# A message-passing layer: three chunks for the last 724 nodes, and rows fetched by SyncE in place of 16 gathered tiles

## The chip, the core and the metric

The kernel runs on one core of one Trainium2 chip. A core has five engines with a queue of instructions each: TensorE (PE, matrix products; PEld is its weight load), VectorE (DVE), ScalarE (ACT), GpSimd (POOL) and SyncE (SP), which only issues transfers and loads registers. The engines run at the same time, each in its own program order, and wait for one another by semaphores. The metric is the device time of one execution in microseconds, the median of several.

## The reference

There are 12500 nodes with 64 features and 212500 edges, sorted by destination, with 32 features each. What is computed, cut to its core:

```python
msg_in = concatenate([nodes[row], nodes[col], edge_features], axis=-1)   # 64 + 64 + 32
messages = relu(msg_in @ mW1 + mb1) @ mW2 + mb2
aggregated = segment_sum(messages, col, num_segments=12500)
upd = relu(concatenate([nodes, aggregated], axis=-1) @ uW1 + ub1) @ uW2 + ub2
out = layernorm(x + upd)        # per node, eps 1e-5, no scale or shift
```

## The kernel before, in words

All is float32. The edges are taken in 554 groups of 384 (three tiles of 128). For a group GpSimd gathers the source rows of its edges from HBM, one indirect transfer per tile (`gather`, L193), 16 groups ahead of their use into a ring of 20. Beside the rows VectorE writes a one-hot of each edge's destination within a window of 32 nodes (`onehot`, L430).

One **step** of the main loop (`for k in range(G)`) does three things on TensorE, for three different groups: it transposes the rows and one-hots of group k (`turn`, L456), makes the hidden layer of group k - 3 (`hidden`, L482, with weights that hold the window's node terms) and sums the hidden rows of group k - 6 by destination (`sums`, L514). ScalarE copies the transposed block to SBUF, with the sums of the older group in the same instruction (L469); in the last ten steps the sums are copied by themselves (L524). VectorE applies the relu (L493).

Every eighth group is not gathered at all (`COPIED`): 48 of its columns a step are copied from a transposed node table in SBUF, half by VectorE (L666), half by ScalarE (L668).

SyncE issues, in each step, the load of the window's weights four steps ahead of the loop and so seven ahead of `hidden` (`window`, L420) and the store of a group's window sums, 64 rows of 129 numbers (`store`, L445). Every fourth step it loads eight window addresses into registers (L410) and the edge features of four groups (`inputs`, L381); every eighth step a list of columns (`indexes`, L624). The stores go by turns to two tables in HBM.

Nodes are **updated** in chunks. `plan` lists chunks of 512 nodes, each with the group after which no edge to it is left, and one last chunk of 212. Once the sums are `SETTLED` groups past that, `step_update` runs one link of the chunk's chain per group: fetch its rows of both tables (`found`, L536), an idle link, transpose and add the counts (L546) and copy them (L556), the same for the sums (L546, L566), the inner product (L572 to L574), relu (L579), the outer product with the node itself (L586, L588), mean and variance (L595, L596), root (L602), scale (L607, L610) and the output's transfer (L615). All its products use one PSUM buffer (`ups`, one deep). After the loop the links that are left run one after another; the last chunk has all of its links there. Its 212 nodes are taken as 106 partitions by 2.

A stream of rows is prepared in the code before, and is empty: `STREAMS = ()`, so `BY_ROWS` has no groups and `row_numbers` and `row_fetch` do nothing. A second program for inputs that do not fit the plan is behind a branch and is not run here.

Of the kernel before, what the change touches and what calls it, by code (L numbers as in the profile page):

```python
# [10 lines left out]
F32 = mybir.dt.float32  # L11
# [3 lines left out]
AF = mybir.ActivationFunctionType  # L15
# [5 lines left out]
P = 128  # L21
N = 12500
E = 212500
D = 64
DE = 32
H = 128
# [3 lines left out]
W = 32  # L30
TG = 3
GE = TG * P
G = (E + GE - 1) // GE
# [9 lines left out]
ROW = H + 1  # L43
STORED = 2 * W
NT = (E + P - 1) // P
NP = N + 44
CH = 512
# [15 lines left out]
ROW_LEAD = 3  # L63

# [31 lines left out]
BY_ROWS = []  # L96
for _, rate, _ in STREAMS:
    BY_ROWS.append([])
# [9 lines left out]
class Own:  # L108
# [26 lines left out]
def ordered(ctx: ExitStack, tc: tile.TileContext, a, own, ok):  # L135
# [3 lines left out]
    nc = tc.nc  # L139
    x, out = a["x"], a["out"]  # L140
# [4 lines left out]
    ups = ctx.enter_context(tc.tile_pool(name="upd_ps", bufs=1, space=PSUM))  # L145
# [3 lines left out]
    ident, wm = own.ident, own.wm  # L149
    xc = own.xc  # L150
# [65 lines left out]
    eps = const.tile([P, 1], F32, name="eps")  # L216
# [104 lines left out]
    wc = const.tile([H, H], F32, name="wc")  # L321

    store_at, rows_at, indices, columns_by = {}, {}, {}, {}
    rows_by, row_index = {}, {}
    fetched = [[] for _ in STREAMS]
    issuers = {"SP": (nc.sync, ET.SP), "PE": (nc.tensor, ET.PE)}
    x_bytes = x.bitcast(U8).rearrange("n b -> (n b)")
    by_dst = dram.tile([NP, H], F32, name="by_dst")
    tables = [dram.tile([NP + STORED, ROW], F32, name=f"by_node{i}") for i in range(2)]
# [196 lines left out]

        return did, [*relu_by[g], *copy_by[g], *([emptied] if emptied else [])], moved

    def update(base, p, n):

        rows, q = slice(base, base + p * n), p * n

        def found():
            parts = [found_p.tile([P, 4, ROW], F32, name=f"found{i}") for i in range(2)]
            for t, table in zip(parts, tables):
                nc.sync.dma_start(t[:p, :n], table[rows, :].rearrange("(n p) w -> p n w", p=p))  # L536
            return parts

        def settled(parts):
            return parts  # L540

        def joined(parts, w, rows_out):
            ps = ups.tile([H, CH], F32, name="u_ps")[:rows_out]
            for k in range(n):
                for i, t in enumerate(parts):
                    nc.tensor.matmul(ps[:, k * p : (k + 1) * p], t[:p, k, w], ident[:p, :p],  # L546
                                     start=i == 0, stop=i == 1)
            return ps

        def counts(parts):  # L550
            return parts, joined(parts, slice(H, ROW), 1)

        def count_moved(got):
            parts, ps = got
            count = up.tile([1, CH], F32, name="count")
            nc.scalar.activation(count[:, :q], ps[:, :q], AF.Copy)  # L556
            return parts, count

        def all_sums(got):
            parts, count = got  # L560
            return joined(parts, slice(0, H), H), count

        def moved(got):
            ps, count = got
            agg = up.tile([H, CH], F32, name="agg")
            nc.vector.tensor_copy(agg[:, :q], ps[:, :q])  # L566
            return agg, count

        def inner(moved_to):
            agg, count = moved_to  # L570
            u_ps = ups.tile([H, CH], F32, name="u_ps")
            nc.tensor.matmul(u_ps[:, :q], wc, agg[:, :q], start=True, stop=False)  # L572
            nc.tensor.matmul(u_ps[:, :q], per_edge, count[:, :q], start=False, stop=False)  # L573
            nc.tensor.matmul(u_ps[:, :q], ux, xc[: D + 1, rows], start=False, stop=True)  # L574
            return u_ps

        def relu(u_ps):
            u = up.tile([H, CH], F32, name="u")
            nc.scalar.activation(u[:, :q], u_ps[:, :q], AF.Relu)  # L579
            return u  # L580

        def outer(u):
            y = ups.tile([H, CH], F32, name="u_ps")[:, : 4 * D].rearrange("p (n d) -> p n d", n=4)
            for k in range(n):
                at = k * p
                nc.tensor.matmul(y[:p, k], xc[: D + 1, base + at : base + at + p], same,  # L586
                                 start=True, stop=False)
                nc.tensor.matmul(y[:p, k], u[:, at : at + p], u2, start=False, stop=True)  # L588
            return y

        def stats(y):
            parts = up.tile([P, 4, nc.vector.BN_STATS_DIM], F32, name="stats")
            mv = up.tile([P, 4, nc.vector.BN_AGGR_DIM], F32, name="mv")
            for k in range(n):
                nc.vector.bn_stats(parts[:p, k], y[:p, k])  # L595
                nc.vector.bn_aggr(mv[:p, k], parts[:p, k])  # L596
            return y, mv

        def root(ym):
            y, mv = ym  # L600
            rstd = up.tile([P, 4], F32, name="rstd")
            nc.scalar.activation(rstd[:p, :n], mv[:p, :n, 1], AF.Sqrt, bias=eps[:p])  # L602
            return y, mv, rstd

        def scaled(ymr):
            y, mv, rstd = ymr
            nc.vector.reciprocal(rstd[:p, :n], rstd[:p, :n])  # L607
            o = up.tile([P, 4, D], F32, name="o")
            for k in range(n):
                nc.vector.tensor_scalar(  # L610
                    o[:p, k], y[:p, k], mv[:p, k, 0:1], rstd[:p, k : k + 1],
                    ALU.subtract, ALU.mult,
                )
            queue = nc.scalar if base + q == N else nc.sync
            queue.dma_start(out[rows, :].rearrange("(n p) d -> p n d", p=p), o[:p, :n])  # L615

        return [found, settled, counts, count_moved, all_sums, moved, inner, relu, outer, stats, root, scaled]

    def indexes(i):

# [58 lines left out]
    def row_span(n, i):  # L679

        _, rate, steps = STREAMS[n]
        size = ROW_TURNS * rate * steps
# [16 lines left out]
    def row_numbers(n, k):  # L699

        _, rate, steps = STREAMS[n]
        q, r = divmod(k - BEGIN, steps)
# [16 lines left out]
    def row_fetch(n):  # L719

        for q, at in [fetched[n].pop(0) for _ in fetched[n][: STREAMS[n][1]]]:
# [4 lines left out]
            after(i, *([] if p else sided(g)))  # L726
            rows_by.setdefault(g, []).append(i)

    waiting = [(closes, update(base, p, n)) for base, p, n, closes in PLAN]
# [38 lines left out]
    def stored():  # L768

        while unstored:  # L770
            store(unstored.pop(0))
# [4 lines left out]
    weights(SB)  # L776
    inputs(0)
    zeroed()
    projected(0)
    projected(1)  # L780
# [415 lines left out]
```

## Time and profile before

| | |
|---|---|
| median of 3 runs | 1881.22 us (1880.9 to 1882.45) |
| the profiled execution | 1878.41 us |
| its span, first to last instruction | 1876.7 us |
| busy: TensorE, VectorE, ScalarE, GpSimd | 1495.1, 1362.5, 1619.6, 1385.6 us |
| gathers (L193) | 1466, 945 ns each |
| mean granted clock of TensorE | 0.938 |

Busy shares are means over the run and hide the gaps between two instructions that an engine spends on issuing: GpSimd's 74% is not 26% of waiting. SyncE's issues are not counted as busy at all; they stand in the timeline with the letter q (SPq, ACTq), with start and length, and what ended a wait stands in the view of waits. A row of the windows gives the window, its length, then for the chosen line the busy time and the number of instructions, the granted clock, the share of the DMA engines and GB/s.

### The profile page before, as it was taken

The numbers are of one execution on the slowest core, as the hardware profiler recorded it, in microseconds if no ns is written. First come the engines' busy times: TensorE is split into PE (matmuls) and PEld (weight loads), VectorE is DVE, ScalarE is ACT, GpSimd is POOL, SyncE is SP. The second block draws the span as 40 slices with busy tenths as digits, with TensorE's granted clock in tenths as the row PEclk, the third lists the DMA queues.
The fourth block names the chain that finished last, engine by engine and source line by source line (L and its number), as shares of the span: only waits on it lengthen the run. The fifth ranks groups of instructions, "written<-read, shape, count | busy, mean of one in ns | idle before, by whom it ended". The sixth has DMA issues, their size and how long they took to land. (4 is left out here: it accounts for less than half of the span.)

```text
span 1876.7 us, 66058 instructions
## 1 busy us (share of the span) xinstructions
PE 1495.1 (80%) x13157; PEld 1217.2 (65%) x13157; DVE 1362.5 (73%) x14069; ACT 1619.6 (86%) x13169; POOL 1385.6 (74%) x1473
## 2 busy tenths in 40 slices
PE   4777888888788778787787878878878878788785
PEld 4666666676676666666675666767656756666673
DVE  3346888888888887877777778778777777787731
ACT  3368999999999999999999999989999898999830
POOL 7777777777777777777777777777777777777770
PEclk9888999999999999999999989989989899999897
DMA  5544333333333333333333333333332323333330
GB/s 136 130 109 93 62 74 74 64 75 74 64 72 74 65 74 68 63 71 71 63 68 68 65 71 64 69 71 60 72 73 63 71 60 72 70 63 72 71 70 17
DMA packets 195851, 135.48 MB, mean 72 GB/s; under 512 B 61029, under 2 KB 170650, under 8 KB 195434
## 3 DMA queue, kind: packets, MB, share of 16 engines
q1 hardware_dynamic: 147678, 82.58, 19.0%
q0 software_dynamic: 46912, 48.10, 14.4%
q14 instruction: 307, 2.51, 0.5%
q8 instruction: 110, 1.80, 0.4%
q10 hardware_dynamic: 844, 0.48, 0.1%
HBM read 103.03 MB, written 27.95 MB: 70 GB/s over the span
## 5 line engine op out<-in xcount | busy, mean ns | idle before, releaser
L193 POOL DMA_INDIRECT own_rows<-in_x,src_sb x1466 | 1384.8, 945 | 447.9 <-issue 178.6
L668 ACT ACTIVATE own_operands<-own_xc 64x1 f32 x12480 | 1295.1, 189 | 28.4 <-issue 6.7
L666 DVE COPY own_operands<-own_xc 64x1 f32 x12480 | 893.7, 136 | 283.4 <-issue 177.5
L456 PE MATMUL own_ps<-own_ident,own_rows 128*96 128x128 f32 x1661 | 299.2, 292 | 302.6 <-ACT own_operands L668 109.6
L482 PE MATMUL own_pre<-own_wm,own_operands 128*128 128x128 f32 x3322 | 492.4, 288 | 0.0
L514 PE MATMUL own_ps<-own_h,own_rows 128*32 128x128 f32 x3322 | 482.3, 284 | 0.0
L456 PEld LDWEIGHTS own_ps<-own_ident,own_rows 128*96 128x96 f32 x1661 | 171.2, 132 | 424.7 <-ACT own_operands L668 205.4
L482 PEld LDWEIGHTS own_pre<-own_wm,own_operands 128*128 128x128 f32 x3322 | 444.3, 203 | 2.4 <-issue 1.6
L469 ACT ACTIVATE own_operands<-own_ps 96x513 f32<-96x513 f32 (+2 forms) x554 | 321.8, 581 | 129.5 <-PE own_ps L514 108.0
L493 DVE TENSOR_SCALAR own_h<-own_pre 128x384 f32<-128x384 f32 x553 | 300.1, 543 | 172.4 <-PE own_ps L514 134.7
L514 PEld LDWEIGHTS own_ps<-own_h,own_rows 128*32 128x32 f32 x3322 | 336.6, 116 | 6.0 <-issue 0.2
L514 PE MATMUL own_ps<-own_one,own_rows 128*32 128x1 f32 x3322 | 199.1, 175 | 3.2 <-ACT own_operands L469 1.7
L514 PEld LDWEIGHTS own_ps<-own_one,own_rows 128*32 128x32 f32 x3322 | 152.3, 114 | 75.3 <-issue 11.4
L430 DVE TENSOR_TENSOR own_rows<-iota,dlc 128x96 f32<-128x96 f32 x554 | 132.4, 240 | 0.0
L546 PE MATMUL u_ps<-own_ident,found 128*1 128x128 f32 (+2 forms) x784 | 110.6, 298 | 19.8 <-SPq L1155 11.2
L546 PEld LDWEIGHTS u_ps<-own_ident,found 128*1 128x1 f32 (+2 forms) x784 | 80.8, 144 | 39.4 <-issue 16.7
L397 PE MATMUL u_ps<-w1b,own_xc 65*128 65x128 f32 x196 | 34.8, 332 | 39.8 <-DMA own_xc<-in_xT 15.5
L397 PEld LDWEIGHTS u_ps<-w1b,own_xc 65*128 65x128 f32 x196 | 29.5, 230 | 45.6 <-issue 25.4
L400 ACT ACTIVATE t<-u_ps 128x512 f32<-128x512 f32 (+1 forms) x25 | 14.6, 586 | 41.1 <-DMA by_dst<-t 17.6
L586 PE MATMUL u_ps<-same,own_xc 65*128 65x64 f32 (+1 forms) x196 | 39.5, 283 | 1.1 <-ACT u L579 1.1
L588 PE MATMUL u_ps<-u,u 128*128 128x64 f32 (+1 forms) x196 | 38.3, 277 | 0.0
L586 PEld LDWEIGHTS u_ps<-same,own_xc 65*128 65x128 f32 (+1 forms) x196 | 29.9, 192 | 7.1 <-ACT own_operands L668 3.4
(69 smaller groups left out, 328.6 us busy)
## 6 DMA issues: line engine op xcount, KB each, us to landing
own_operands<-in_efT SPq DMA_DIRECT2D x138, 192.0 KB
own_rows<-in_x,src_sb POOLq DMA_INDIRECT x1466
by_node<-own_operands SPq DMA_DIRECT2D x554, 32.2 KB
found<-by_node SPq DMA_DIRECT2D x48, 258.0 KB
own_wm<-by_dst SPq DMA_DIRECT2D x554, 16.0 KB
by_dst<-t SPq DMA_DIRECT2D x24, 256.0 KB
out<-o SPq DMA_DIRECT2D x24, 128.0 KB
own_xc<-in_xT SPq DMA_DIRECT2D x12, 179.2 KB
```

Of the source, the lines that this page charges most:

```text
L193: nc.gpsimd.indirect_dma_start(out=s[:p, j, :D], out_offset=None, in_=x[:, :], in_offset=bass.IndirectOffsetOnAxis(ap=src_sb[:p, g * TG + ...
L397: nc.tensor.matmul(ps[:, j], xc[: D + 1, base + j * P :][:, :P], w1b, start=True, stop=True)
L430: places_by[g] = nc.vector.tensor_tensor(own.s[g % RING][:, :, D:], iota.unsqueeze(1).to_broadcast([P, TG, W]), dlc[:, g * TG : (g + 1) * ...
L456: nc.tensor.transpose(xt[:, j * P : j * P + p], sides[g] if g in sides and j == TG - 1 else s[:p, j, :], ident[:p, :p])
L469: after(nc.scalar.activation(t[r, c : c + n], ps[r, :n], AF.Copy), step))]
L482: nc.tensor.matmul(pre[:p, j, :], t[:, c + j * P : c + j * P + p], wm[g % NW], start=True, stop=True)
L493: relu_by[g] = [nc.vector.tensor_scalar(h, pre, 0.0, None, ALU.max)]
L514: did.append(nc.tensor.matmul(out_ps, s[:p, j, D:], of(j, p), start=j == 0, stop=j == len(sizes) - 1))
L546: nc.tensor.matmul(ps[:, k * p : (k + 1) * p], t[:p, k, w], ident[:p, :p], start=i == 0, stop=i == 1)
L586: nc.tensor.matmul(y[:p, k], xc[: D + 1, base + at : base + at + p], same, start=True, stop=False)
L666: by[engine] = nc.vector.tensor_copy(o, x_at)
L668: by[engine] = nc.scalar.activation(o, x_at, AF.Copy)
```

## The change

Two things are changed.

First, the end. `plan` now lists 23 chunks of 512, two of 256 and the last of 212, so the last 724 nodes are three chunks. `SETTLED` is 1 and not 2. The last chunk is taken in pieces of 128 and 84 nodes; both tables get zeros in the 44 rows behind the last node, so that its fetch reads 128 partitions by 2. Its fetch is issued right after the loop, ahead of the links that other chunks have left. It has a shorter chain of its own (`both`, `both_moved`): sums and counts in one link, each in a PSUM bank of its own, taken from the buffers of the loop, and the product with the nodes' own features ahead of those with counts and sums. Its output goes out in two transfers, one from ScalarE's queue and one from SyncE's. For the other chunks the order of the inner product's three parts is changed in the same way.

Second, `STREAMS = (("SP", 4, 2),)`. In each step from 18 on SyncE issues four transfers of one node row (256 bytes) from HBM to a side tile, and every second step it loads eight row addresses into registers. 128 rows make a tile: the third tile of groups 52, 84, and so on to 532, 16 in all, comes from the side tile and isn't gathered. There are two side tiles. VectorE writes a one-hot into the side tile, and turns row numbers into addresses.

```diff
-SETTLED = 2
+SETTLED = 1
-STREAMS = ()
+STREAMS = (("SP", 4, 2),)
...
-    for e in [c * CH for c in range(1, N // CH + 1)] + [N]:
-        n = e - b
-        chunks.append((b, *((P, n // P) if n % P == 0 else (n // 2, 2)),
-                       next((g for g in range(G) if least(g) >= e), G)))
+    whole = N // CH * CH
+    for e in [*range(CH, whole, CH), whole - CH // 2, whole, N]:
+        chunks.append((b, e - b, next((g for g in range(G) if least(g) >= e), G)))
...
+        for table in tables:
+            for n in range(N, NP, W):
+                m = min(W, NP - n)
+                nc.sync.dma_start(table[n : n + m, :],
+                                  own.st[0][D + W : D + W + m, GE : GE + ROW])
...
+        def bank(i):
+            if final:
+                return (*own.pre, *own.ps)[i][:, :CH]
+            return ups.tile([H, CH], F32, name="u_ps")
...
+        def own_inner(ps):
+            nc.tensor.matmul(ps[:, :q], ux, xc[: D + 1, base : base + q], start=True, stop=False)
+            return ps
...
+        def both(parts):
+            ps = joined(parts, slice(0, H), 0)
+            count = joined(parts, slice(H, ROW), 1)
+            return parts, ps, count, own_inner(bank(2))
...
+            u_ps = begun[0] if begun else own_inner(bank(2))
             nc.tensor.matmul(u_ps[:, :q], per_edge, count[:, :q], start=False, stop=False)
-            nc.tensor.matmul(u_ps[:, :q], ux, xc[: D + 1, rows], start=False, stop=True)
+            nc.tensor.matmul(u_ps[:, :q], wc, agg[:, :q], start=False, stop=True)
...
-            queue = nc.scalar if base + q == N else nc.sync
-            queue.dma_start(out[rows, :].rearrange("(n p) d -> p n d", p=p), o[:p, :n])
+            if final:
+                for k, (p, queue) in enumerate(zip(sizes, (nc.scalar, nc.sync))):
+                    queue.dma_start(out[nodes[k], :], o[:p, k])
...
+    _, (find, *others) = waiting.pop()
+    parts = find()
     while now or waiting:
         step_update(G + SETTLED)
+    for other in others:
+        parts = other(parts)
```

What the new `STREAMS` sets going stands in the code before already:

```python
        for n in range(len(STREAMS)):
            row_numbers(n, k)       # every second step: eight addresses into registers
            row_fetch(n)            # four transfers of one row
```

SyncE's queue in the middle of the loop, before (four steps; L420 is a window's weights, L445 a store, L381 the features, L624 a list):

```order
L410 TENSOR_LOAD start_b
L420 DMA own_wm<-by_dst 32x512
L445 DMA by_node_177<-own_operands 64x516
L420 DMA own_wm<-by_dst 32x512
L445 DMA by_node_178<-own_operands 64x516
L381 DMA own_operands<-in_efT 32x4x384
L420 DMA own_wm<-by_dst 32x512
L445 DMA by_node_177<-own_operands 64x516
L624 DMA index<-in_src_copied 1x384
```

And with the change (here L424 is the weights, L449 the store, L753 the load of row addresses, L768 the rows):

```order
L414 TENSOR_LOAD start_b
L424 DMA own_wm<-by_dst 32x512
L449 DMA by_node_177<-own_operands 64x516
L753 TENSOR_LOAD row_index_10246
L768 DMA own_side<-in_x 1x256 x4
L424 DMA own_wm<-by_dst 32x512
L449 DMA by_node_178<-own_operands 64x516
L768 DMA own_side<-in_x 1x256 x4
L385 DMA own_operands<-in_efT 32x4x384
L424 DMA own_wm<-by_dst 32x512
L449 DMA by_node_177<-own_operands 64x516
```

Behind each store now stand four row transfers, and behind every second store a register load too; all that comes after on this queue stands behind them.

SyncE's queue at the end of the run, before (L615 is the output of the chunk ahead of the last, L536 the last chunk's fetch):

```order
L445 DMA by_node_177<-own_operands 64x516
L445 DMA by_node_178<-own_operands 64x516
L615 DMA out<-o 128x4x64
L536 DMA found_94544<-by_node_177 106x2x129
L536 DMA found_94545<-by_node_178 106x2x129
```

And with the change (L555 is the fetch, L656 the output of the second half chunk, L653 a piece of the last output):

```order
L449 DMA by_node_177<-own_operands 64x516
L449 DMA by_node_178<-own_operands 64x516
L555 DMA found_101043<-by_node_177 128x2x129
L555 DMA found_101044<-by_node_178 128x2x129
L656 DMA out<-o 128x2x64
L653 DMA out<-o 84x64
```

The last fetch has changed places with the output ahead of it, and reads 128 partitions and not 106.

More of the change, by code (lines that the diff above doesn't have):

```diff
@@ L527, in sums, with update, reads @@
         return did, [*relu_by[g], *copy_by[g], *([emptied] if emptied else [])], moved
-    def update(base, p, n):
-        rows, q = slice(base, base + p * n), p * n
+    def update(base, q):
+        final = base + q == N
+        n = (q + P - 1) // P
+        sizes = [min(P, q - k * P) for k in range(n)]
+        nodes = [slice(base + k * P, base + k * P + p) for k, p in enumerate(sizes)]
+        columns_of = [slice(k * P, k * P + p) for k, p in enumerate(sizes)]
+        def bank(i):
+            if final:
+                return (*own.pre, *own.ps)[i][:, :CH]
+            return ups.tile([H, CH], F32, name="u_ps")
+        def reads(i):
+            if final:
+                tc.declare_no_dep(i.ins, group="quiet", reason="TensorE's later product is waited for")
         def found():
@@ L535, in found @@
             for t, table in zip(parts, tables):
-                nc.sync.dma_start(t[:p, :n], table[rows, :].rearrange("(n p) w -> p n w", p=p))
+                nc.sync.dma_start(
+                    t[:, :n], table[base : base + n * P, :].rearrange("(n p) w -> p n w", p=P))
             return parts
@@ L555, in count_moved @@
             count = up.tile([1, CH], F32, name="count")
-            nc.scalar.activation(count[:, :q], ps[:, :q], AF.Copy)
+            reads(nc.scalar.activation(count[:, :q], ps[:, :q], AF.Copy))
             return parts, count
@@ L560, in all_sums @@
             parts, count = got
-            return joined(parts, slice(0, H), H), count
+            return joined(parts, slice(0, H), 0), count
         def moved(got):
@@ L578, in relu @@
             u = up.tile([H, CH], F32, name="u")
-            nc.scalar.activation(u[:, :q], u_ps[:, :q], AF.Relu)
+            reads(nc.scalar.activation(u[:, :q], u_ps[:, :q], AF.Relu))
             return u
         def outer(u):
[L583 to L588, printed above, removed]
+            y = rows_of(bank(3))
+            for k, p in enumerate(sizes):
+                nc.tensor.matmul(y[:p, k], xc[: D + 1, nodes[k]], same, start=True, stop=False)
+                nc.tensor.matmul(y[:p, k], u[:, columns_of[k]], u2, start=False, stop=True)
             return y
@@ L593, in stats @@
             mv = up.tile([P, 4, nc.vector.BN_AGGR_DIM], F32, name="mv")
-            for k in range(n):
-                nc.vector.bn_stats(parts[:p, k], y[:p, k])
+            if sizes[-1] < P:
+                nc.vector.memset(mv[:, n - 1], 1.0)
+            for k, p in enumerate(sizes):
+                reads(nc.vector.bn_stats(parts[:p, k], y[:p, k]))
                 nc.vector.bn_aggr(mv[:p, k], parts[:p, k])
@@ L606, in scaled @@
             y, mv, rstd = ymr
-            nc.vector.reciprocal(rstd[:p, :n], rstd[:p, :n])
+            nc.vector.reciprocal(rstd[:, :n], rstd[:, :n])
             o = up.tile([P, 4, D], F32, name="o")
-            for k in range(n):
-                nc.vector.tensor_scalar(
+            for k, p in enumerate(sizes):
+                reads(nc.vector.tensor_scalar(
                     o[:p, k], y[:p, k], mv[:p, k, 0:1], rstd[:p, k : k + 1],
                     ALU.subtract, ALU.mult,
-                )
-            queue = nc.scalar if base + q == N else nc.sync
-            queue.dma_start(out[rows, :].rearrange("(n p) d -> p n d", p=p), o[:p, :n])
-        return [found, settled, counts, count_moved, all_sums, moved, inner, relu, outer, stats, root, scaled]
+                ))
+            if final:
+                for k, (p, queue) in enumerate(zip(sizes, (nc.scalar, nc.sync))):
+                    queue.dma_start(out[nodes[k], :], o[:p, k])
+                assert n <= 2
+            else:
+                nc.sync.dma_start(
+                    out[base : base + q, :].rearrange("(n p) d -> p n d", p=P), o[:, :n])
+        if final:
+            return [found, both, both_moved, inner, relu, outer, stats, root, scaled]
+        return [found, settled, counts, count_moved, all_sums, moved, inner, relu, outer, stats,
+                root, scaled]
     def indexes(i):
@@ L727, in row_fetch @@
             rows_by.setdefault(g, []).append(i)
-    waiting = [(closes, update(base, p, n)) for base, p, n, closes in PLAN]
+    waiting = [(closes, update(base, q)) for base, q, closes in PLAN]
     now = []
```

27 lines of the change are left out of this document (16 added, 11 removed).

## The prediction

> **What bounds the kernel now.** I read the windows first, for two lines of the program: GpSimd's gathers (L193) and ScalarE's copy that ends each step's transposes (L469, one a step).
>
> ```profile
> L193 POOL DMA_INDIRECT own_rows<-in_x,src_sb x1466 | 1384.8, 945 | 447.9 <-issue 178.6
> 200.00:300.00 100.00, 75.62 (x81) 0.98 0.33 69
> 1500.00:1600.00 100.00, 75.55 (x81) 0.93 0.32 65
> ...
> 200.00:300.00 100.00, 19.24 (x34) 0.98 0.33 69
> 1500.00:1600.00 100.00, 17.74 (x31) 0.93 0.32 65
> ...
> 155.00:1757.00 1602.00, 290.67 (x498) 0.95 0.33 69
> 1757.00:1877.00 120.00, 13.51 (x25) 0.85 0.25 51
> ...
> 1332.77 0.95 POOL L193 DMA_INDIRECT own_rows<-in_x,src_sb  x1 [0.30 <-ACT own_operands L469]
> 1833.38 0.90 POOL L193 DMA_INDIRECT own_rows<-in_x,src_sb  x1 [0.30 <-DMA own_rows<-in_x,src_sb]
> ```
>
> The first pair of windows counts gathers: 81 in every 100 us, early and late. With 0.945 us of work and 0.30 us between two, a gather takes 1.245 us, and the last begins at 1833.38: GpSimd never stops, so its queue sets the end of the steps. The second pair counts steps: 34 in 100 us early on (2.94 us each, ScalarE's own pace while it catches up) and 31 later. The third gives 498 steps in 1602 us, 3.22 us each. Eight steps need 21 gathers, 26.1 us or 3.27 a step: GpSimd's pace. ScalarE could do about 3.0.
>
> The other engine that the change touches is SyncE. Its own waits between 200 and 1800 us:
>
> ```profile
> SPq L445 <- ACT own_operands L469: 595.6, 385, 4.9
> SPq L615 <- DVE o L610: 74.1, 20, 4.4
> SPq L445 <- DMA found<-by_node: 40.1, 25, 4.2
> ```
>
> SyncE has room: 710 us of these 1600 are waiting, most of it for ScalarE's copy before a store. So it works at most 1.8 us a step (890 us by 498 steps). The question is what four more transfers a step make of that.
>
> **The change, part by part.** *Gathers.* 16 of 1466 go: 16 x 1.245 = 19.9 us off GpSimd's queue, 83 gathers instead of 84 in 32 steps, or 3.23 us a step. That is the whole gain of this part, and it is only had while nothing else needs more than 3.23.
>
> *SyncE's steps.* Each of 512 steps (18 to 529) issues four row transfers, and every second one loads eight row addresses into registers; 17 small transfers bring the lists. No row transfer stands in the trace, so I price it by the nearest issues on the same queue.
>
> ```profile
> 17.57 1.76 SPq L420 DMA_DIRECT2D own_wm<-by_dst  x4
> 19.38 0.41 SPq L783 DMA_DIRECT2D dlc_i<-in_dst_cols  x1
> ...
> 25.09 0.32 SPq L624 DMA_DIRECT2D index<-in_src_copied  x1
> 25.45 0.36 SPq L254 DMA_DIRECT2D src_sb<-in_src  x1
> ...
> 1320.83 0.48 SPq L445 DMA_DIRECT2D by_node<-own_operands  x1
> 1322.50 0.32 SPq L420 DMA_DIRECT2D own_wm<-by_dst  x1
> ...
> 1325.37 0.97 SPq L536 DMA_DIRECT2D found<-by_node  x2
> 1326.44 0.44 SPq L420 DMA_DIRECT2D own_wm<-by_dst  x1
> ...
> 1330.02 0.57 SPq L381 DMA_DIRECT2D own_operands<-in_efT  x1
> 1330.69 0.38 SPq L420 DMA_DIRECT2D own_wm<-by_dst  x1
> 1331.25 0.48 SPq L445 DMA_DIRECT2D by_node<-own_operands  x1
> 1331.83 0.53 SPq L420 DMA_DIRECT2D own_wm<-by_dst  x1
> 1332.65 0.48 SPq L445 DMA_DIRECT2D by_node<-own_operands  x1
> 1333.81 0.32 SPq L420 DMA_DIRECT2D own_wm<-by_dst  x1
> ```
>
> A row transfer, from start to start: at most 0.45 us (four transfers whose address is in a register, 17.57 to 19.38), at least 0.36 (a transfer of a single row to the next one, 25.09 to 25.45, address fixed). The register costs the difference seen at 1330.69 (0.10 us after the issue before it) against 1330.02 beside it (0.07 or less). I take 0.40: the single row plus about 0.04. Four are 1.60.
>
> The rest, per step, with SyncE never waiting: the store 0.48 and the 0.15 us ahead of it (0.18 before 1331.25) = 0.63; the window's weights 0.32 and 0.15 = 0.47, since they then stand behind a row and not behind a store (0.32 against the 0.53 at 1331.83); 0.20 for the first row where it stands right behind the store, every second step = 0.10. A register load: the gap of 0.68 us ahead of 1333.81, less the usual 0.11 = 0.57, and at 1322.50 a gap of 1.19, so 1.08. For the rows one every second step, at 0.57 = 0.29 (0.54 at the other end); the one already there, every fourth step = 0.21. Features every fourth step, 0.64 = 0.16; index lists 0.09; a chunk's two fetches and its output, some 1.6 us in 22.6 steps = 0.07; the store that waits for a chunk's fetch, 40.1 us over 490 steps = 0.08, which stays. Sum 3.70 us a step. With a row at 0.36, no 0.20 and 0.05 less on each of the two other gaps: 3.34. With a row at 0.45 and the loads at 1.08: 4.15.
>
> So SyncE needs 3.70 us where GpSimd allows 3.23, and **SyncE becomes the bound.** What is late then: the weights of a window (asked for seven steps ahead of the product that reads them), the rows (due three steps after the last is issued) and a chunk's sums. TensorE waits for these, ScalarE and VectorE wait for TensorE, GpSimd for ScalarE's copy 20 groups back. SyncE never waits long, because what it waits for was done a step ago.
>
> [...]
>
> *The start and the end of the steps.* First the stores of SyncE that mark the pace of the first steps, then the tail, then a fetch of a whole chunk early in the run.
>
> ```profile
> 55.72 0.55 SPq L445 DMA_DIRECT2D by_node<-own_operands  x1
> 154.16 0.48 SPq L445 DMA_DIRECT2D by_node<-own_operands  x1
> ...
> 1833.86 0.49 PE L456 MATMUL own_ps<-own_ident,own_rows 128*96 128x128 f32 x3
> 1836.56 0.43 PE L456 MATMUL own_ps<-own_ident,own_rows 128*96 128x128 f32 x2
> 1842.48 0.27 ACT L524 ACTIVATE own_operands<-own_ps 32x129 f32<-32x129 f32 x1 [3.87 <-PE own_ps L514]
> 1851.43 0.40 SPq L615 DMA_DIRECT2D out<-o  x1
> 1851.94 1.11 SPq L536 DMA_DIRECT2D found<-by_node  x2
> 1857.29 0.51 PE L546 MATMUL u_ps<-own_ident,found 106*1 106x106 f32 x2 [9.05 <-SPq L1155]
> 1859.91 1.22 PE L546 MATMUL u_ps<-own_ident,found 106*1 106x106 f32 x6 [2.11 <-SPq L1155]
> 1871.30 0.52 ACTq L615 DMA_DIRECT2D out<-o  x1
> ...
> 239.78 0.39 SPq L536 DMA_DIRECT2D found<-by_node  x1
> 243.31 0.74 PEld L546 LDWEIGHTS u_ps<-own_ident,found 128*1 128x1 f32 x8 [0.36 <-DMA found<-by_node]
> ```
>
> The last sums are copied by 1842.75. The final fetch is issued at 1851.94 only, behind the output of the chunk ahead of it. Moved ahead, it waits just for the last store: 0.5 us of issue and about 2 us of landing (estimate), so 1845.3. Its two halves now land 5.3 and 8.0 us after issue (1857.29, 1859.91); a fetch in 128 partitions landed 3.5 us after issue (239.78 to 243.31). TensorE would start at about 1849.5 instead of 1859.91: 10 us. The chain to the output, 11.4 us, loses about 1 (count and sums in one go, the copies beside products). The output itself takes 5.4 us to the end of the span, in 106 partitions; in two pieces perhaps 3. Together 14 us (8 to 17): about 26 us from the last transposes (1836.5) to the end, where now it is 40. The half chunk before it costs one more chain of eleven steps, all but its last steps beside group work.
>
> [...]
>
> **Sum.** SyncE issues the 20th store, that of step 25, at 154.16. Steps 18 to 24 add rows while it already waits in line for node tables: 7 x 2.0 = 14 us. Steps 25 to 529: 505 x 3.70 = 1869. TensorE is then some four steps ahead; of the 20 steps left, ten at ScalarE's 3.0 and ten short ones at 2.7 (the transposes at 1833.86 and 1836.56) = 57. Then 26. Together 2120 us of span. What lies around the span is 1.7 us (1878.4 against 1876.7), and the median lies 2.8 above the profiled execution: 2124, against 1881.2 now, 13% slower. VectorE's extra one-hot (0.24 us in 32 steps, L430) and address product lie beside other work; without that cover they are 4 us.
>
> **Rivals.** *SyncE keeps up* (the other side: faster). If a row costs 0.28 us or less, the step's sum is 3.23, GpSimd stays the bound and the gathers saved count: 1878.4 - 19.9 - 14 + 2.8 = 1847 us. For it: SyncE waits 710 us of 1600 now. Against: no issue in the view is shorter than 0.29 and none starts closer to the next than 0.36. [...] Chance 0.13.
>
> *SyncE is bound by a little*: row near 0.32, step 3.3, so 505 x 3.3 in the sum above = 1922 us. Chance 0.06.
>
> *The rows land late*, with SyncE keeping up: each of 16 tiles stops the transposes for up to one step of 3.2 us, 51 us at most, 1847 + 51 = 1898. It needs a landing longer than three steps, 9.7 us, and the longest in the view is 8.0. Chance 0.02.
>
> *Much dearer*: rows at 0.45 and loads at 1.08, 4.15 a step, 2351 us; chance 0.05 for more than 2270.
>
> **How the numbers follow.** Forecast, SyncE the bound at 3.34 to 4.0 us a step: 0.74. A measurement here can tell 0.2%, 4 us, from no change. Slower is the forecast, the dear end, the little and half of the late rows (0.74 + 0.05 + 0.06 + 0.01 = 0.86); the other half of the late rows is no change (0.01); faster 0.13. The range: 3.34 a step gives 1942 and 4.0 gives 2275; I take 1915 to 2270, which takes in the bound by a little and leaves out 0.2.
>
> **What would show it.** SyncE's waits for ScalarE's copy nearly gone; steps per 100 us down from 31 to 27; row issues 0.40 us apart; GpSimd with gaps, waiting for ScalarE; TensorE waiting for window weights, rows and sums. At the end the fetch within 3 us of the last sums and under 4 us to land. The forecast is wrong if gathers still come at 81 in 100 us, or if rows are under 0.3 us apart.

## The result and the profile after

The changed kernel takes 2048.62 us (median of 5 runs, 2046.06 to 2052.05), the kernel before 1881.22 (5 runs). The ratio is 1.089 [1.0875, 1.0905]: 8.9% slower, where 13% was forecast. The span of the profiled execution grew from 1876.7 to 2044.3 us, by 167.6. Cut at two places that both traces have, SyncE's 20th store and the start of the last copy of sums by ScalarE, it divides like this:

| stretch of the span | before | after | difference |
|---|---|---|---|
| to the 20th store | 154.2 | 159.1 | +5.0 |
| to the last copy of sums | 1688.3 | 1865.2 | +176.9 |
| to the end | 34.2 | 20.0 | -14.2 |

So the end became shorter, about as the forecast had it, and the steps paid for it twelve times over. The windows count them: first the gathers (now L192), then ScalarE's copies, one a step (now L473); a row gives the window, its length, busy time and count, granted clock, DMA share, GB/s.

```profile
300.00:500.00 200.00, 137.87 (x147) 0.90 0.29 62
1000.00:1200.00 200.00, 137.89 (x147) 0.92 0.29 63
...
300.00:500.00 200.00, 33.20 (x57) 0.90 0.29 62
1000.00:1200.00 200.00, 33.29 (x57) 0.92 0.29 63
```

Before, GpSimd began 81 gathers in every 100 us; now it begins 73.5, though it has fewer to do. There are 57 steps in 200 us, 3.5 us each, where there were 61 to 66. What the engines wait for stands in the view of all waits, first two rows of before, then the changed kernel:

```profile
POOL own_rows L193 <- ACT own_operands L469: 37.5, 123, 0.3
...
PE u_ps L546 <- DMA found<-by_node: 7.5, 6, 5.5
```

```profile
DVE own_h L497 <- PE own_ps L518: 307.2, 81, 15.8
POOL own_rows L192 <- ACT own_operands L473: 195.8, 175, 8.1
...
PE u_ps L566 <- DMA found<-by_node: 169.0, 43, 12.5
...
PE own_ps L460 <- DMA own_side<-in_x: 45.4, 8, 9.9
```

GpSimd waits 195.8 us for ScalarE's copy to free a place in its ring (37.5 before), ScalarE and VectorE wait for TensorE, and TensorE waits for two things that SyncE issues: a chunk's sums (169.0 us, 43 times, up to 12.5; 7.5 us before) and the fetched rows (45.4 us, 8 times). And SyncE, between 200 and 1800 us:

```profile
SPq L449 <- ACT own_operands L713: 50.7, 133, 1.4
SPq L449 <- DMA found<-by_node: 39.0, 20, 3.3
SPq L449 <- ACT own_operands L473: 23.0, 57, 1.0
```

Of the 595.6 us that it waited for ScalarE's copy before a store, 23.0 are left (and 50.7 for the column copies that ScalarE does behind it); all rows of this view together are 140 us where they were 795. SyncE has become the queue that sets the pace. Some three steps of it, from the timeline (start, length, engine and line, transfer):

```profile
1310.93 0.48 SPq L449 DMA_DIRECT2D by_node<-own_operands  x1
1312.55 1.25 SPq L768 DMA_DIRECT2D own_side<-in_x  x4
1314.02 0.96 SPq L555 DMA_DIRECT2D found<-by_node  x2
1315.14 0.38 SPq L424 DMA_DIRECT2D own_wm<-by_dst  x1
1318.15 0.48 SPq L449 DMA_DIRECT2D by_node<-own_operands  x1
1318.74 1.35 SPq L768 DMA_DIRECT2D own_side<-in_x  x4
1321.08 0.32 SPq L424 DMA_DIRECT2D own_wm<-by_dst  x1
1321.49 0.48 SPq L449 DMA_DIRECT2D by_node<-own_operands  x1
1322.67 1.23 SPq L768 DMA_DIRECT2D own_side<-in_x  x4
1324.06 0.32 SPq L424 DMA_DIRECT2D own_wm<-by_dst  x1
```

The four rows take 1.23 to 1.35 us. Loads of eight row addresses show as the gaps ahead of 1312.55 (1.14 us) and 1322.67 (0.70), against 0.11 ahead of the rows at 1318.74 where no load stands; the gap of 0.99 ahead of 1321.08 is the load of window addresses. The view of a line's instructions gives their durations, in ns the shortest, the median and the longest:

```profile
L753 SPq TENSOR_LOAD <-row_index x256: 523/536/991, 123.9 to 1941.2; - x128
...
L768 SPq DMA_DIRECT2D own_side<-in_x x2048: 224/225/388, 124.9 to 1945.4; - x187
```

The chunk's fetch at 1314.02 is one of those that TensorE waits for; the store at 1318.15 waits for it too. The products that read it, and ScalarE's copies around it:

```profile
1317.14 0.59 PE L566 MATMUL u_ps<-own_ident,found 128*1 128x128 f32 x2 [9.12 <-DMA found<-by_node]
...
1311.20 0.58 ACT L473 ACTIVATE own_operands<-own_ps 96x513 f32<-96x513 f32 x1
1323.88 0.59 ACT L473 ACTIVATE own_operands<-own_ps 32x513 f32<-32x513 f32 x1 [1.99 <-PE own_ps L518]
```

The products start 3.1 us after the fetch was issued; the fetch of the kernel before that the prediction shows took 3.5. So it was issued late, and did not land more slowly. For 12.7 us no step ends. In the 15 us ahead of this halt ScalarE makes a step in 2.85 to 3.1 us. So in this trace the saturated SyncE doesn't look like a steady slow step: the engines run ahead at their old pace, run dry at the next chunk or side tile, and halt until SyncE has caught up.

The end, from the timeline:

```profile
2024.35 0.27 ACT L528 ACTIVATE own_operands<-own_ps 32x129 f32<-32x129 f32 x1 [2.08 <-PE own_ps L518]
2025.22 1.71 SPq L555 DMA_DIRECT2D found<-by_node  x2
2029.55 3.35 PE L566 MATMUL own_pre<-own_ident,found 128*128 128x128 f32 x16
2037.54 0.39 ACTq L653 DMA_DIRECT2D out<-o  x1
2037.78 0.39 SPq L653 DMA_DIRECT2D out<-o  x1
```

The last fetch is issued 0.9 us after the last copy began (9.5 before), and the products that read both tables start 5.2 us after that copy (17.4 before, with two of them 2.6 us earlier): 12 us saved there. They start without a wait, behind the half chunk's products. From the first output's issue to the end at 2044.3 it is 6.8 us.

### The profile page after: what moved, and what is told of

Read it like the earlier page. It is cut to its first block, busy times and chain, and to the rows that moved or that the text cites. A ratio compares the mean times of both kernels' runs of the same rounds, so it can differ in the third digit from the quotient of the medians.

```text
span 2044.3 us, 70810 instructions
## 1 busy us (share of the span) xinstructions
PE 1528.3 (75%) x13163; PEld 1227.7 (60%) x13163; DVE 1365.8 (67%) x14121; ACT 1617.4 (79%) x13172; POOL 1370.4 (67%) x1457
## 5 line engine op out<-in xcount | busy, mean ns | idle before, releaser
L192 POOL DMA_INDIRECT own_rows<-in_x,src_sb x1450 | 1369.6, 945 | 589.6 <-issue 251.1
L518 PE MATMUL own_ps<-own_h,own_rows 128*32 128x128 f32 x3322 | 477.0, 282 | 0.0
L473 ACT ACTIVATE own_operands<-own_ps 96x513 f32<-96x513 f32 (+2 forms) x554 | 321.6, 581 | 177.5 <-PE own_ps L518 156.3
L566 PE MATMUL u_ps<-own_ident,found 128*1 128x128 f32 (+1 forms) x768 | 131.7, 334 | 169.0 <-DMA found<-by_node 169.0
L566 PEld LDWEIGHTS u_ps<-own_ident,found 128*1 128x1 f32 (+1 forms) x768 | 83.1, 150 | 212.5 <-DMA found<-by_node 173.0
L583 ACT ACTIVATE count<-u_ps 1x512 f32<-1x512 f32 (+1 forms) x25 | 14.1, 566 | 137.2 <-PE u_ps L566 137.2
L401 PEld LDWEIGHTS u_ps<-w1b,own_xc 65*128 65x128 f32 x196 | 30.2, 235 | 46.9 <-issue 27.4
L622 PE MATMUL u_ps<-same,own_xc 65*128 65x64 f32 x192 | 38.5, 282 | 0.5 <-ACT u L616 0.5
L623 PE MATMUL u_ps<-u,u 128*128 128x64 f32 x192 | 37.4, 277 | 0.0
```

Source lines behind the costliest of these rows:

```text
L192: nc.gpsimd.indirect_dma_start(out=s[:p, j, :D], out_offset=None, in_=x[:, :], in_offset=bass.IndirectOffsetOnAxis(ap=src_sb[:p, g * TG + ...
L401: nc.tensor.matmul(ps[:, j], xc[: D + 1, base + j * P :][:, :P], w1b, start=True, stop=True)
L473: after(nc.scalar.activation(t[r, c : c + n], ps[r, :n], AF.Copy), step))]
L518: did.append(nc.tensor.matmul(out_ps, s[:p, j, D:], of(j, p), start=j == 0, stop=j == len(sizes) - 1))
L566: nc.tensor.matmul(ps[:, k * P : (k + 1) * P], t[:, k, w], ident, start=j == 0, stop=j == 1)
L622: nc.tensor.matmul(y[:p, k], xc[: D + 1, nodes[k]], same, start=True, stop=False)
```

## The experiments

Two theories. **Theory A**: SyncE's own time a step is the bound, and this time is a sum of prices over what it issues. **Rival B**: SyncE has the time, but its rows land late. Five runs vary the rows; seven more fell on two slower chips and stand behind them, among them three kernels that vary the end.

**Rows fetched and not read.** All 1466 tiles are gathered as before the change, and SyncE fetches its rows as in the change; the rows that it fetches are read by nobody and waited for by nobody.

```diff
-            if g not in columned and (j < TG - 1 or g not in sides)
+            if g not in columned
...
-                sides[g] if g in sides and j == TG - 1 else s[:p, j, :], ident[:p, :p])
+                s[:p, j, :], ident[:p, :p])
```

> The changed kernel, but all 1466 gathers are made and the transposes read the gathered tile and don't wait for the rows. SyncE still issues the 2048 row transfers and loads their addresses, and nobody reads what they bring (the side tiles). Theory (SyncE's issue time is the bound): as slow as the changed kernel, 2035 to 2055 us, and the 16 gathers matter nothing. Rival (rows that land late stop the transposes): TensorE's 45 us of waiting for rows and what hangs on them go, and GpSimd's pace comes back: 1870 to 1990.

Measured: 2048.26 us, 1.0873 [1.0851, 1.0895] times the kernel before. TensorE's wait for a chunk's sums, then SyncE's for ScalarE's copy between 200 and 1800 us:

```profile
PE u_ps L566 <- DMA found<-by_node: 235.7, 47, 14.3
...
SPq L449 <- ACT own_operands L473: 14.6, 41, 0.5
```

With no one waiting for rows the time is that of the change, so Rival B falls as a cause of the loss: the 45.4 us in which TensorE waited for rows are one form that the lateness takes, and without them it waits 66.7 us longer for sums. The 16 gathers saved are worth next to nothing either while SyncE is the bound. What this run leaves open is whether the row transfers, read or not, hold up other transfers; the last of the five runs answers that.

**Two rows a step**, eight addresses every fourth step; eight tiles come from rows, not 16.

```diff
-STREAMS = (("SP", 4, 2),)
+STREAMS = (("SP", 2, 4),)
```

> The changed kernel with two rows a step and a load of eight addresses every fourth step: 8 tiles, not 16. Theory: SyncE's step falls from 3.56 by two rows at 0.35 and a quarter of a load of 0.8, to 2.66 us, under GpSimd's 3.25, so the loss is gone whole: 1867 - 8 x 1.245 = 1857 us, 1850 to 1864. Rival (each row costs its part, wherever SyncE stands): half the loss, about 1955.

Measured: 1861.84 us, 0.9879 [0.9856, 0.9901]: 1.2% faster than the kernel before, and the best here. Its gathers in windows, then SyncE's largest wait between 200 and 1800 us:

```profile
300.00:500.00 200.00, 151.09 (x160) 0.98 0.31 71
1000.00:1200.00 200.00, 151.17 (x161) 0.96 0.30 68
```

```profile
SPq L449 <- ACT own_operands L473: 163.5, 186, 5.1
```

GpSimd is at its 80 a 100 us again and SyncE waits for ScalarE again. Two rows and half the loads less turn the loss of 167 us into a gain, and the rival's half of the loss is not there: Theory A in its main part. The new end and the earlier start of the chunks are in this kernel too, so they alone do not make the loss.

**Three rows a step**, six addresses every second step.

```diff
-STREAMS = (("SP", 4, 2),)
+STREAMS = (("SP", 3, 2),)
```

> The changed kernel with three rows a step and a load of six addresses every second step: 12 tiles. Theory: SyncE's step is 3.56 - 0.35 = 3.21 us against GpSimd's 3.24, at the edge: 1852 (no loss, 12 gathers saved) to 1900 (small stalls at the chunks), I say 1872. Rival (each row costs its part): three quarters of the loss, about 2002.

Measured: 2012.94 us, 1.0677 [1.0659, 1.0695]: the forecast of 1872 is missed by 141 us. The line's view shows where the row that was saved went:

```profile
L753 SPq TENSOR_LOAD <-row_index x256: 746/1239/1294, 124.8 to 1910.3; - x128
```

Three rows take 0.98 us on the average where four took 1.30, 0.32 less. But a load of six addresses lasts 1.24 us (median), where those of eight in the changed kernel last 0.53 and 0.97 by turns. Over 300 to 1700 us the mean gap between a store and the rows behind it is 0.71 us and was 0.47: 0.24 us a step given back, and the step is 3.48 us where it was 3.54. The rival's 2002 us is near the time measured; the last of the five runs tells the two apart.

**Sixteen addresses a load**, every fourth step, with four rows a step.

```diff
-STREAMS = (("SP", 4, 2),)
+STREAMS = (("SP", 4, 4),)
```

> The changed kernel with its four rows a step, but 16 addresses loaded every fourth step and not eight every second. Theory: SyncE's time is a plain sum, and a load costs about 0.8 us (gaps of 0.7 and 1.1 us in the changed kernel's trace): one load less in four steps is 0.15 to 0.2 us a step, 75 to 100 us over 512 steps: 1950 to 1975. Rival (the transfers alone set the pace, loads lie beside them): 2040 to 2055.

Measured: 2041.83 us, 1.0839 [1.0817, 1.086]: missed again, by some 70 us. The loads:

```profile
L753 SPq TENSOR_LOAD <-row_index x128: 973/1418/1453, 122.8 to 1925.8; - x128
```

A load of sixteen lasts 1.42 us, 0.35 a step; two loads of eight in four steps, one cheap and one dear, are 0.53 + 0.97 = 1.50, or 0.37 a step. So next to nothing is saved. The time lies in the rival's range, and this run alone does not refute it. By the durations in the traces, in both misses it was not the sum that failed but the price of a load, which I had taken to be the same whatever its length.

**Three rows, loads of eight.** To show that the load, and not the third row, made the run with three rows slow: eight addresses are loaded and six of them used (the list holds two that are not used behind every six).

```diff
+LOADED = 8
...
-                row_index[n, i][0:1, b : b + some], engines=[issuers[STREAMS[n][0]][1]],
+                row_index[n, i][0:1, b : b + LOADED], engines=[issuers[STREAMS[n][0]][1]],
...
-            fetched[n].extend(enumerate(v, q * rate * steps))
+            fetched[n].extend(enumerate(v[:some], q * rate * steps))
```

> Three rows a step, as in the run with three rows, but each load takes eight addresses of which six are used. Theory (the load of six addresses was dear by itself, 1.25 us, where a load of eight takes 0.57 or about 1.0): the step is the changed kernel's 3.54 less one row of 0.33 = 3.21 us, about GpSimd's own 3.23, so about 1870 us (1852 to 1900). Rival (the dear load comes with three rows and not with the number six, or the loads vary for a reason outside the program): loads again at 1.25 us, step 3.48, 2000 to 2015 us.

Measured: 1912.3 us, 1.0153 [1.0128, 1.0178]. Two more addresses in each load make the kernel 100 us faster, with the same 1536 row transfers. Its loads, its gathers in a window, and SyncE's largest wait between 200 and 1800 us:

```profile
L753 SPq TENSOR_LOAD <-row_index x256: 523/540/1005, 124.5 to 1806.6; - x128
```

```profile
1000.00:1200.00 200.00, 151.44 (x160) 0.96 0.32 69
...
SPq L450 <- ACT own_operands L714: 64.8, 160, 1.5
```

The loads are back at 0.53 and 0.97 us by turns: they were dear as they were laid out, six at a time, and not because of three rows. The same transfers at 2013 and at 1912 us also mean that it isn't by crowding other transfers that the rows cost this time, and that loads do not lie beside the transfers at no cost: the rivals of the two runs above fall. The time is 12 us beyond the forecast's upper end, with a step of 3.30 us (from the first row's issue to the last) and not 3.21. GpSimd makes 160 gathers in 200 us, near its 162, and SyncE waits 64.8 us for ScalarE's column copies where it was 50.7. That two queues of almost the same pace hold each other up now and then is my reading of this, not tested apart.

**Seven runs fell on two chips where the kernel before itself takes 2632 and 2676 us** (TensorE's granted clock was about 0.79 there). A step lasts some 4.6 us on them without any rows, so a fuller queue has little to lose there, and the size of the loss on the other chips can't be read from them. ScalarE's steps in a window and SyncE's wait for its copy between 300 and 1700 us, first with the end alone, then with the rows alone:

```profile
1000.00:1200.00 200.00, 25.74 (x44) 0.78 0.23 49
...
SPq L449 <- ACT own_operands L473: 542.5, 205, 5.7
```

```profile
1000.00:1200.00 200.00, 25.83 (x44) 0.77 0.21 46
...
SPq L445 <- ACT own_operands L469: 18.8, 37, 1.5
```

SyncE's waits go there too: it is about full at 4.6 us a step, and with the rows alone four rows last 1.8 us on the mean (1.3 in the changed kernel on its chip). Why these chips are slower no run shows.

The two halves of the change alone: the end without rows (the changed kernel with `STREAMS = ()`, on either chip), and the rows without the new end (the kernel before with `STREAMS = (("SP", 4, 2),)`).

> The changed kernel with the row stream left empty, so only the new end of the run is in it. My theory (SyncE's issues make the whole loss, the new end gains): in the changed kernel's trace 19.7 us lie between the last copy of sums (2024.62) and the end of the span, against 33.9 before (1842.75 to 1876.7), so 1881 - 14 = 1867 us, 1862 to 1872; gathers at 81 in 100 us as before. Rival: the third chunk and the earlier links lengthen the steps by as much as the end saves: 1878 to 1884.

> The kernel before with the stream of four rows a step alone, old end. Theory: the whole loss comes from SyncE, so the changed kernel's time plus the 14 us of the end: 2063 us, 2052 to 2072, with 3.5 to 3.6 us a step between steps 18 and 529. Rival: the loss needs the other edits too (chunks started one group earlier, so that TensorE reaches their sums before the fetch has landed): under 2000 us.

Measured: the end alone 2631.3 us, 0.9993 [0.997, 1.0015], and on the other chip 2668.93, 0.9966 [0.9944, 0.9988]; the rows alone 2677.4, 1.0171 [1.0127, 1.0216].

From the last copy of sums to the end of the span the end alone takes 24.3 us on the first chip and the old end, with the rows alone, 37.8: 13.5 less, close to the 14.2 of the change. But the whole run with the end alone is only 2 us shorter on that chip (the interval goes from 8 shorter to 4 longer) and 9 on the other (3 to 15). So the rival of the first expectation, that the steps lose what the end saves, is not refuted on these chips. On the others only the run with two rows bears on it: its tail is 22.5 us and was 34.2, its eight tiles are worth 10, and it lies 21.8 us below the kernel before on its own chip (1883.63), about the sum of the two. That the loss of the rows needs other edits of the change too, the rival of the second, is untried at four rows.

The sizes expected could not be tried on the slower chips. Nor could those of two more runs: three rows with loads of eight (2679.7, 1.0011 [0.9986, 1.0035]), the kernel that took 1912.3 us above, and four rows without any load of addresses (2713.45, 1.0138 [1.0086, 1.019]). The latter gathers all tiles and fetches the same eight rows again in every two steps, which nobody reads, so that SyncE loads addresses once.

> Three rows a step as in the run that came out at 2013 us, but the list of rows is laid out so that each load brings eight addresses to registers, of which six are used. In the run with six addresses a load took 1.35 us of gap, each time; eight addresses take 0.7 or 1.1. Theory (SyncE's time is a plain sum of its issues and loads): 3.54 - 0.32 for the row = 3.22 us a step, under GpSimd's 3.24 by a hair: 1852 to 1900 us, I say 1870. Rival (a stream costs what it costs by the number of its transfers or by what lands late, loads don't matter): 2000 to 2015.

> As the run with rows that nobody reads (all gathers made, 2048 us), but the eight addresses are loaded once and used for all 2048 row transfers; no later loads and no lists. The rows fetched are thus the same eight again and again, into the side tiles that nobody reads. Theory of the plain sum: 3.55 - 0.38 for the loads - 0.03 for the lists = 3.14 us a step of SyncE, under GpSimd's 3.27: 1865 to 1900 us. Rival (four transfers a step are too many by themselves): 1990 to 2045.

What can be compared on such a chip is the end, among three kernels without rows: the new end, the new end with its fetch behind the links left over from other chunks, and the new end with 106 partitions by 2 for the last 212 nodes.

```diff
-    parts = find()
     while now or waiting:
         step_update(G + SETTLED)
+    parts = find()
```

```diff
-        sizes = [min(P, q - k * P) for k in range(n)]
+        w = q // 2 if final else P
+        sizes = [w] * n
```

> As the run with the end alone, but the last chunk's fetch is issued behind the links that the half chunk has left, as it was before. Theory: the links left take some 7 us (2024.2 to 2031.1 in the changed kernel's trace), and the fetch and its landing then stand alone: 5 to 7 us slower than with the end alone, about 1873. Rival: the fetch waits for the last stores anyway and its place is worth under 1 us: 1867.

> As the run with the end alone, but the last 212 nodes stand in 106 partitions by 2, for the fetch, the products, and the output (two transfers of 106 rows). Theory: the two fetches landed 5.3 and 8.0 us after issue in 106 partitions before, and not later than 4.3 us after issue in 128, so TensorE starts 2 to 4 us later: 1869 to 1871. Rival: the landing is hidden beneath the half chunk's links, which hold TensorE until then: within 1 us of the end alone.

Measured: 2634.0 us, 1.0007 [0.9985, 1.0028], and 2636.6, 1.0009 [0.999, 1.0029], beside 0.9993 [0.997, 1.0015] for the new end: medians 2.7 and 5.3 us apart, within the intervals. The traces tell more. The new end:

```profile
2604.50 0.27 ACT L528 ACTIVATE own_operands<-own_ps 32x129 f32<-32x129 f32 x1 [2.08 <-PE own_ps L518]
2605.37 1.68 SPq L555 DMA_DIRECT2D found<-by_node  x2
2610.20 3.81 PE L566 MATMUL own_pre<-own_ident,found 128*128 128x128 f32 x16
```

With the fetch behind the links:

```profile
2612.79 0.27 ACT L528 ACTIVATE own_operands<-own_ps 32x129 f32<-32x129 f32 x1 [2.07 <-PE own_ps L518]
2620.52 0.92 SPq L555 DMA_DIRECT2D found<-by_node  x2
2622.88 3.87 PE L566 MATMUL own_pre<-own_ident,found 128*128 128x128 f32 x16 [4.88 <-DMA found<-by_node]
```

With 106 partitions:

```profile
2602.12 0.27 ACT L528 ACTIVATE own_operands<-own_ps 32x129 f32<-32x129 f32 x1 [2.08 <-PE own_ps L518]
2602.99 1.57 SPq L556 DMA_DIRECT2D found<-by_node  x2
2611.67 3.12 PE L567 MATMUL own_pre<-own_ident,found 106*128 106x106 f32 x14 [1.89 <-DMA found<-by_node]
```

From the last copy of sums to the end of the span the three take 24.3 us (to 2628.8), 27.1 (to 2639.9) and 27.4 (from 2602.12 to 2629.5). The fetch's place moves the products by 4.4 us (5.7 after the last copy, or 10.1) and the end by 3; the 128 partitions, for fetch, products and output together, are worth 3 as well: with 106 the second table is there 8.7 us after issue, with 128 both are there after 4.8 at most. These are single traces, on a slow chip, and the medians do not confirm the 3 us.

## Why the prediction was right, and where it was off

**SyncE becomes the bound: right.** SyncE's waits for the copy nearly gone, GpSimd with gaps and waiting for ScalarE, TensorE waiting for sums and rows: all of it stands in the trace, and the runs with unread rows, with two rows, and with three rows at two prices of a load show that SyncE's own time and not a landing is the cause. One item of that list is not there: after 161 us TensorE never waits for a window's weights (6.6 us in three waits ahead of that, 9.7 in the whole kernel before), so seven steps of lead were enough. And one of the two signs of being wrong came close: rows start 0.33 us apart (median), and the sign was 0.3.

**The size: 2044.3 us of span and not 2120.** By the prediction's own terms:

| term | predicted | measured | difference |
|---|---|---|---|
| 20th store, with 14 us for steps 18 to 24 | 168.2 | 159.1 | -9 |
| steps 25 to 529, 505 x 3.70 or 3.54 | 1868.5 | 1786.5 | -82 |
| the steps left, to the last transposes | 57 | 74.5 | +17.5 |
| from there to the end | 26 | 24.2 | -2 |

The term that was off is the price of SyncE's step, and in it one row. Over 300 to 1700 us (395 steps, 3.54 us each), each item with the time ahead of it:

| us a step | predicted | measured |
|---|---|---|
| four rows | 1.70 | 1.30 + 0.12 = 1.42 |
| load of row addresses | 0.29 | 0.40 |
| store, with what it waits | 0.63 + 0.08 = 0.71 | 0.51 + 0.25 = 0.76 |
| weights | 0.47 | 0.34 + 0.17 = 0.51 |
| load of window addresses | 0.21 | 0.21 |
| features, lists, chunks | 0.32 | 0.25 |
| sum (before rounding) | 3.70 | 3.54 |

A row's issue lasts 0.225 us, and with the time ahead of each a row costs 1.42 / 4 = 0.36 us; I had 0.40 (0.425 with the extra for a store ahead), and 0.36 as the lower bound. What I added to that bound, for the register and for a store ahead, was too much, and the price of such an issue isn't fixed. The same list of columns, in the kernel before (right behind a store) and with the change (behind rows):

```profile
L624 SPq DMA_DIRECT2D index<-in_src_copied x65: 287/415/462, 25.1 to 1735.6; - x65
```

```profile
L669 SPq DMA_DIRECT2D index<-in_src_copied x65: 230/231/327, 27.0 to 1923.1; - x65
```

The issue behind rows is the cheaper one here, 0.23 us against 0.42 (medians), and three of the four rows stand behind a row. Behind a store the four last 1.34 us and behind a load 1.25 (medians), so about 0.04 a step where 0.10 was set. The features, too, stand behind rows now, and the item with them came out 0.07 under. The loads erred the other way, by 0.11: 0.57 was the price of the cheaper half, and the dearer half lies near the other end that I had named.

The 14 us for the first steps were too much. 5 were seen, and with two rows a step the 20th store stands at 159.1 as well, so it is hardly a price by the row; that the rows fit into the waits for node tables is my reading. The last steps took 17 us more than forecast: 22 and not 20 were left after the last row, and the transposes first waited 7.2 us for that last side tile.

**The end: right in sum, not in parts.** 14 us were forecast and 14.2 came. The fetch brought 12 and not 10 (the landing of the last store, 2 us by the prediction's estimate, came out near that: 1.9 us from the store's issue at 2024.64 to that of the fetch that waited for it, and 2.1 and 2.4 at the chunk fetches of 239.78 and 308.86 in the kernel before); the chain from there to the output's issue takes 8.0 us and not 11.4, 3.4 less where 1 was forecast; the output, for which I guessed 3 us, takes 6.8 in two pieces, where 5.4 were seen before. That the sum came out right is luck. The traces of the three kernels that vary the end put about 3 us on the fetch's place and 3 on the partitions, with the half chunk in all three; the rest is then the half chunk and the shorter chain, which no run separates.

**SyncE keeps up (rival, 0.13): false at four rows, true at two.** Its price of entry, 3.23 us a step, fits the runs: with two rows the kernel came out at 1861.84, where eight tiles saved at 1.245 us and 14 us of the end give 1881.2 - 10 - 14 = 1857; with three and loads of eight, whose sum was put at 3.21, it nearly kept up. Starting 2048 transfers of 256 bytes, 0.36 us each and the loads beside it, is what the 8.9% went into. The rows landing late (0.02) is refuted as the cause, and the bound "by a little" and the "much dearer" case lie on either side of what came.

## What to carry to other kernels

SyncE's queue took 3.54 us a step with four rows, where GpSimd's pace was 3.23. Add up such a price, register loads included, before giving a queue more, and compare it with the pace of the engine that is to be relieved. The waits of SyncE were the room that there was: 595.6 us over 498 steps, 1.2 us a step, enough for two rows and not for four, which took 1.8 with their loads. Where several engines halt in bursts on late transfers (here TensorE 169.0 us for sums and 45.4 for rows, ScalarE and VectorE behind it), look for one issuing queue without waits behind all of them, and test with transfers that nobody waits for.

## What the runs showed of the hardware

- A load of addresses into SyncE's registers did not get dearer in proportion to their number. Of eight it took 0.53 and 0.97 us by turns in the changed kernel, of six 1.24 (median), of sixteen 1.42. The loads of eight window addresses in the kernel before have the same two prices, and the last of them, of four, lasted 0.30. With two rows a step, loads of eight are nearly all dear (0.96 to 1.00 for the 33 between 300 and 700 us). The window addresses before, then the row addresses with two rows:

```profile
L410 SPq TENSOR_LOAD <-start_b x139: 300/532/1027, 15.2 to 1819.9; - x139
...
L753 SPq TENSOR_LOAD <-row_index x128: 523/972/1011, 126.0 to 1739.4; - x128
```

  Why six cost more than eight, and why the loads of eight differ, stays open. No run separates the number from the place: six begin at every 24 bytes of the list, eight at every 32. In the changed kernel the loads of eight window addresses last 0.78 (median, 0.52 to 1.03).
- An issue of one row of 256 bytes with its address in a register lasts 0.225 us (median of 2048, changed kernel), and another row in a series adds some 0.32 (four last 1.30 us, the three of the run with three rows 0.98).
- Two of the four chips that the experiments ran on took 1.4 times as long for the same program (2632 and 2676 us, TensorE's granted clock about 0.79), and on the first of them the rows alone cost 1.7%, where the whole change cost 8.9% elsewhere. The loss was the smaller where a step without rows lasted longer: some 4.6 us there, 3.22 in the kernel before of the prediction.
